# Counting edges in a metaformer kernel: stationary and moving operand exchanged, even and odd columns of words in the two column halves of the array

## The chip, the cores and the metric

The kernel runs on one core of a Trainium2 chip. The metric is the device time of one execution in microseconds (us); less is better. The core has a matrix engine (PE, with its weight loads shown as PEld), a vector engine (DVE), an engine for activations and copies (ACT), a general engine (POOL), and a sync engine (SP) that mostly issues DMAs. Each engine works through its own instructions strictly in the order in which they were written for it; engines wait for each other through semaphores.

## What is computed

The reference is a network of two layers on an image x of shape (2, 64, 64, 256): layer 0 is a deformable attention and a mixture of four experts whose router is a graph attention over 1,048,576 edges; layer 1 is a window attention and a mixture of eight experts. The part that matters here is the graph attention:

```python
M = 2 * 4096                      # 8192 nodes that exist
src = edge_index[0]; dst = edge_index[1]     # drawn from 0 .. 65535
e = leaky_relu(a_src[src] + a_dst[dst], 0.2)
ee = exp(e - e_max[dst])
denom = segment_sum(ee, dst, num_segments=M)
agg = segment_sum(h[src] * alpha[:, :, None], dst, num_segments=M)
```

Node numbers reach beyond the 8192 nodes that exist. A source out of range is read as the last node, M - 1; an edge whose destination is out of range adds to no sum. So seven of eight sources are the same node, and all edges with that source and one destination carry the same message. It is enough to count them per destination: the router multiplies the last node's message by `count`.

## The kernel before

**Stages.** `static_maps` (0 to about 990 us) computes the query, key, value and offset maps of layer 0: projections and transposes on PE (L245, L251), depthwise convolutions of queries and values on DVE (L205, L207), of keys on PE (L349), offsets on PE (L372, L373), transposes of values (L297). `static_attention` follows from 991 us with the dot products (L473) and the weighted sums (L733 to L746). Then come the router, the experts of layer 0, the attention of layer 1 and its experts.

**Sorting and counting.** `sort_edges` is a generator that `static_maps` steps through while it writes its own work, so the sorting lies among the maps of layer 0. A scheduler then fixes one order per engine. The 1,048,576 edges lie as 128 partitions of 8192 columns, taken in 16 chunks of 512 columns. Per chunk two DMAs load sources and destinations (L1077, L1078). DVE packs each edge with a destination that exists into one 32-bit word (L1079 to L1083), and picks the 56 greatest words of each 256 columns and partition, eight at a time (L1088, L1089). That makes 112 columns of words per chunk, 1792 in all (`NW`).

**One-hot products.** Bits 0 to 6 of a word are the low part of the destination (`lob`), bits 7 to 12 the high part (`hib`); a word that is no edge of the last node, or empty, gets 512 or more added to the high part and so matches nothing. For 16 columns of words (`JC`) DVE writes two one-hot tiles in bfloat16 in one instruction each: `ol` [128, 128, 16] (L1115) and `oh` [128, 64, 16] (L1116), from buffers of which there are two each. The column of words is the last index, so the operand of one column, `ol[:, :, j]`, takes every 16th element. PE then multiplies them, one matmul per column of words, all into one sum:

```python
psc = pp.tile([P, NT], F32, name="psc")          # [128, 64]
nc.tensor.matmul(
    psc, lhsT=ol[:, :, j], rhs=oh[:, :, j], start=(c1 == 0), stop=(c1 == NW - 1),
)
```

`lhsT` is the stationary operand, loaded as weights; `rhs` moves through the array. Contraction runs over the 128 partitions, so `psc[low, high]` grows by the number of words with that destination. At the end DVE copies `psc` to `count` (L1123) and goes on with the choice of the words that are not counted (L1125 to L1157: L1132 and L1133 pick the front words, L1147 finds the greatest left).

**Shape of the array.** A float32 matmul runs as two passes. The profile names for each PE instruction the shape in which the array is used, rows*columns: 128*128 for the projections, convolutions, offsets, transposes and the counting before the change; 64*64 for the small products of the offset weights (L895); 32*64 for L473; 128*64 for the logits of layer 1 (L1830), whose output goes by turns to partitions 0 to 63 and 64 to 127.

Of the kernel before, what the change touches and what calls it, by code (L numbers as in the profile page):

```python
# [23 lines left out]
F32 = mybir.dt.float32  # L24
I32 = mybir.dt.int32
AF = mybir.ActivationFunctionType
ALU = mybir.AluOpType
# [4 lines left out]
P = 128  # L32
# [3 lines left out]
NT = M // P  # L36
# [104 lines left out]
class Net:  # L141
# [905 lines left out]
    def sort_edges(self, one):  # L1047

        tc, nc, I = self.tc, self.nc, self.I
        es = I["edges"][0].rearrange("(p j) -> p j", p=P)
        ed = I["edges"][1].rearrange("(p j) -> p j", p=P)
        BF = mybir.dt.bfloat16
        NS = NCOL // SUBC  # L1060
        NW = NS * SUBK
        INSIDE = float(np.array([WORD | M], np.int32).view(np.float32)[0])
        count, front, left, dealt, rounds = one
        with tc.tile_pool(name="se1", bufs=1, side="right") as op, tc.tile_pool(name="se2", bufs=2, side="right") as wp, \
                tc.tile_pool(name="seps", bufs=1, space=PSUM, side="right") as pp:
            iota = op.tile([P, P], F32, name="iota")
            nc.gpsimd.iota(iota, [[1, P]], base=0, channel_multiplier=0, allow_small_or_imprecise_dtypes=True)
            number = op.tile([P, P, JC], BF, name="number")
            nc.vector.tensor_copy(number, iota.unsqueeze(2).to_broadcast([P, P, JC]))
            first = op.tile([P, NS, SUBK], F32, name="first")  # L1070
            rest = op.tile([P, NCOL // CHUNK + 4], F32, name="rest")
            psc = pp.tile([P, NT], F32, name="psc")
            c1 = 0
            for c0 in range(0, NCOL, CHUNK):
                si = wp.tile([P, CHUNK], I32, name="si")
                di = wp.tile([P, CHUNK], I32, name="di")
                nc.sync.dma_start(si, es[:, c0 : c0 + CHUNK])  # L1077
                nc.sync.dma_start(di, ed[:, c0 : c0 + CHUNK])  # L1078
                nc.vector.tensor_scalar(si, si, M - 1, None, ALU.min)  # L1079
                nc.vector.tensor_scalar(si, si, 13, WORD | (M - 1) << 13, ALU.logical_shift_left, ALU.bitwise_xor)  # L1080
                nc.vector.tensor_tensor(si, si, di, ALU.bitwise_or)
                wf = wp.tile([P, CHUNK], F32, name="wf")
                nc.vector.scalar_tensor_tensor(wf, di, float(M), si.bitcast(F32), ALU.is_lt, ALU.mult)  # L1083
                for k in range(CHUNK // SUBC):
                    part = wf[:, k * SUBC : (k + 1) * SUBC]
                    at = c0 // SUBC + k
                    for r in range(0, SUBK, 8):
                        nc.vector.max(first[:, at, r : r + 8], part)  # L1088
                        nc.vector.match_replace(part, first[:, at, r : r + 8], part, 0.0)  # L1089
                nc.vector.tensor_reduce(rest[:, c0 // CHUNK : c0 // CHUNK + 1], wf, AX.X, ALU.max)  # L1090
                nc.sync.dma_start(left[:, c0 : c0 + CHUNK], wf)


                n = CHUNK // SUBC * SUBK
                words = first[:, c0 // SUBC : c0 // SUBC + CHUNK // SUBC, :].rearrange("p a b -> p (a b)")
                wi = words.bitcast(I32)
                lo = wp.tile([P, n], I32, name="lo")
                hi = wp.tile([P, n], I32, name="hi")
                nc.vector.tensor_scalar(lo, wi, P - 1, None, ALU.bitwise_and)
                nc.vector.tensor_scalar(hi, wi, 7, NT - 1, ALU.logical_shift_right, ALU.bitwise_and)  # L1100
                lob = wp.tile([P, n], BF, name="lob")
                nc.vector.tensor_copy(lob, lo)

                other = wp.tile([P, n], F32, name="other")
                nc.vector.tensor_scalar(other, words, INSIDE, 512.0, ALU.is_ge, ALU.mult)
                hib = wp.tile([P, n], BF, name="hib")
                nc.vector.tensor_tensor(hib, other, hi, ALU.add)
                nc.vector.tensor_scalar(other, words, 0.0, 512.0, ALU.is_equal, ALU.mult)
                nc.vector.tensor_tensor(hib, other, hib, ALU.add)
                for j0 in range(0, n, JC):  # L1110
                    ol = wp.tile([P, P, JC], BF, name="ol")
                    oh = wp.tile([P, NT, JC], BF, name="oh")
                    lj = lob[:, j0 : j0 + JC].unsqueeze(1)
                    hj = hib[:, j0 : j0 + JC].unsqueeze(1)
                    nc.vector.tensor_tensor(ol, lj.to_broadcast([P, P, JC]), number, ALU.is_equal)  # L1115
                    nc.vector.tensor_tensor(oh, hj.to_broadcast([P, NT, JC]), number[:, 0:NT, :], ALU.is_equal)  # L1116
                    for j in range(JC):
                        nc.tensor.matmul(  # L1118
                            psc, lhsT=ol[:, :, j], rhs=oh[:, :, j], start=(c1 == 0), stop=(c1 == NW - 1),
                        )  # L1120
                        c1 += 1
                yield
            nc.vector.tensor_copy(count, psc)  # L1123
            ff = first.rearrange("p a b -> p (a b)")
            nc.vector.scalar_tensor_tensor(ff, ff, INSIDE, ff, ALU.is_ge, ALU.mult)  # L1125
            inner = op.tile([P, NS, SUBIN], F32, name="inner")
            nc.vector.tensor_copy(inner, first[:, :, 0:SUBIN])
            nc.vector.memset(first[:, :, 0:SUBIN], 0.0)
            nf = inner.rearrange("p a b -> p (a b)")
            more = op.tile([P, SPREAD + SPARE], F32, name="more")  # L1130
            for r in range(0, KEEP, 8):
                nc.vector.max(front[:, r : r + 8], nf)  # L1132
                nc.vector.match_replace(nf, front[:, r : r + 8], nf, 0.0)  # L1133
            for r in range(0, SPREAD + SPARE, 8):
                nc.vector.max(more[:, r : r + 8], nf)
                nc.vector.match_replace(nf, more[:, r : r + 8], nf, 0.0)

            nc.sync.dma_start(dealt, more[:, 0:SPREAD])
            hand = op.tile([P, SPREAD], F32, name="hand")
            nc.sync.dma_start(hand, dealt.rearrange("p c -> (p c)").rearrange("(j q) -> q j", q=P))  # L1140
            for r in range(KEEP, FRONT, 8):
                nc.vector.max(front[:, r : r + 8], hand)
                nc.vector.match_replace(hand, front[:, r : r + 8], hand, 0.0)
            at = NCOL
            for i, words in enumerate((ff, nf, hand, more[:, SPREAD:])):
                n = words.shape[1]
                nc.vector.tensor_reduce(rest[:, NCOL // CHUNK + i : NCOL // CHUNK + i + 1], words, AX.X, ALU.max)  # L1147
                nc.sync.dma_start(left[:, at : at + n], words)
                at += n
            top = op.tile([P, 1], F32, name="top")  # L1150
            nc.vector.tensor_reduce(top, rest, AX.X, ALU.max)
            topa = op.tile([P, 1], F32, name="topa")
            nc.gpsimd.partition_all_reduce(topa, top, P, bass_isa.ReduceOp.max)
            nc.vector.tensor_scalar(rounds, topa[0:1, :], 0.0, float(NLEFT), ALU.is_gt, ALU.mult)
# [1176 lines left out]
```

## Time and profile before

| what | us |
|---|---|
| median of 5 runs | 6423.25 (6404.69 to 6434.82) |
| the profiled execution's own time | 6407.83 |
| its span, first to last instruction | 6406.0 |
| PE busy | 5043.2 |
| DVE busy | 3726.7 |
| ACT busy | 1440.7 |
| POOL busy | 2263.9 |
| counting matmuls L1118, 1792 of them, busy | 239.1 |
| one-hot tiles `ol` L1115, 112 of 1.223 | 137.0 |
| one-hot tiles `oh` L1116, 112 of 0.683 | 75.5 |
| copy of the counts L1123 | 0.224 |
| key convolutions on PE L349, busy | 264.5 |
| offsets on PE L372, busy | 177.2 |
| projections on PE L251, busy | 179.8 |

How to read it: the engines work side by side, so busy times do not add up to the span. A group of instructions is a line of the kernel, an engine, an operation and the tiles it writes and reads. The duration of a matmul is from its start until its result stands; matmuls overlap in the array, so the pace of a row of them is the distance from start to start. Idle time before an instruction is put down to what released it: "DVE ol L1115 <- PE psc L1118" is DVE waiting at L1115 for the matmuls of L1118. The granted clock of PE is given as a share of full speed; it averages 0.84 over the span and is 1.00 or 0.50 at any moment of it.

### The profile page before, as it was taken

The numbers are of one execution on the slowest core, as the hardware profiler recorded it, in microseconds if no ns is written. First come the engines' busy times: TensorE is split into PE (matmuls) and PEld (weight loads), VectorE is DVE, ScalarE is ACT, GpSimd is POOL, SyncE is SP. The second block draws the span as 40 slices with busy tenths as digits, with TensorE's granted clock in tenths as the row PEclk, the third lists the DMA queues.
The fourth block names the chain that finished last, engine by engine and source line by source line (L and its number), as shares of the span: only waits on it lengthen the run. The fifth ranks groups of instructions, "written<-read, shape, count | busy, mean of one in ns | idle before, by whom it ended". The sixth has DMA issues, their size and how long they took to land. (4 is left out here: it accounts for less than half of the span.)

```text
span 6406.0 us, 68586 instructions
## 1 busy us (share of the span) xinstructions
PE 5043.2 (79%) x23911; PEld 3020.3 (47%) x23911; DVE 3726.7 (58%) x6085; ACT 1440.7 (22%) x2580; POOL 2263.9 (35%) x1994
## 2 busy tenths in 40 slices
PE   9999985698899898998772667089966777769983
PEld 5646783333334343333341333078843444448872
DVE  7797775567888888899551448012135555532223
ACT  3221112223333332310030000022213444312210
POOL 0000000247777687798417440700034111110025
PEclk9899985578898898998895878599977878879996
DMA  4446666545555555642430000267732000048875
GB/s 155 151 131 147 107 47 149 115 97 145 117 138 131 135 140 140 139 102 60 103 66 6 4 4 1 102 222 225 224 115 63 20 20 21 20 144 261 262 238 154
DMA packets 946767, 740.49 MB, mean 116 GB/s; under 512 B 611794, under 2 KB 833246, under 8 KB 935264
## 3 DMA queue, kind: packets, MB, share of 16 engines
q1 hardware_dynamic: 725004, 488.35, 30.3%
q10 hardware_dynamic: 185812, 167.81, 9.7%
q0 software_dynamic: 35584, 79.71, 4.2%
q8 instruction: 197, 3.23, 0.2%
q14 instruction: 170, 1.39, 0.1%
HBM read 469.87 MB, written 276.15 MB: 116 GB/s over the span
## 5 line engine op out<-in xcount | busy, mean ns | idle before, releaser
L746 PE MATMUL acc<-prod,ident 128*128 128x512 f32 x2716 | 1389.6, 657 | 156.5 <-POOL prod L740 129.5
L733 DVE TENSOR_TENSOR prod<-vt,wp 128x1536 f32<-128x1536 f32 (+1 forms) x796 | 1334.6, 1734 | 210.7 <-PE acc L746 156.2
L740 POOL TENSOR_TENSOR prod<-prod 128x512 f32<-128x512 f32 x1010 | 1305.9, 1316 | 418.3 <-DVE prod L733 397.8
L746 PEld LDWEIGHTS acc<-prod,ident 128*128 128x128 f32 x2716 | 524.2, 205 | 822.6 <-issue 547.5
L480 ACT COPY stage<-dot 128x384 f32<-128x384 f32 (+1 forms) x640 | 482.4, 840 | 1073.0 <-PE dot L473 905.2
L473 PE MATMUL dot<-kt,qt 32*64 32x192 f32 (+1 forms) x5888 | 514.4, 417 | 154.9 <-ACT stage L480 86.3
L1501 PE MATMUL ps_h<-xgT,w1t 128*128 128x256 f32 x2240 | 552.6, 395 | 49.1 <-DVE xgT L1496 16.7
L1234 PE MATMUL ps<-oh,ol 128*128 128x512 f32 (+1 forms) x864 | 362.2, 583 | 252.8 <-DVE oh L1227 152.0
L473 PEld LDWEIGHTS dot<-kt,qt 32*64 32x64 f32 x5888 | 281.3, 165 | 546.5 <-ACT stage L480 267.7
L1509 PE MATMUL ps_y<-w2t,hT 128*128 128x256 f32 x2240 | 512.8, 383 | 0.0
L1512 DVE TENSOR_TENSOR y<-ps_y,b2t 128x256 f32<-128x256 f32 x280 | 118.9, 425 | 654.7 <-PE ps_y L1509 494.4
L1501 PEld LDWEIGHTS ps_h<-xgT,w1t 128*128 128x128 f32 x2240 | 421.3, 195 | 133.3 <-DVE xgT L1496 27.6
L1509 PEld LDWEIGHTS ps_y<-w2t,hT 128*128 128x128 f32 x2240 | 431.7, 193 | 59.4
L1504 ACT ACTIVATE hT<-ps_h,b1t 128x256 f32<-128x256 f32 x560 | 258.3, 473 | 854.8 <-PE ps_h L1501 781.2
L1234 PEld LDWEIGHTS ps<-oh,ol 128*128 128x128 f32 x864 | 180.8, 213 | 433.9 <-issue 333.8
L2127 POOL DMA_INDIRECT xs<-tn,sloti x128 | 124.3, 971 | 646.4 <-DVE slot L2125 553.6
L1596 POOL DMA_INDIRECT back<-ys,back_row x128 | 123.2, 963 | 621.7 <-DVE run L2112 549.5
L207 DVE SCALAR_TENSOR_TENSOR cv<-pad,colt,cv 128x2048 f32<-128x2048 f32 x128 | 296.8, 2345 | 0.0
L349 PE MATMUL ps_k<-padk,diag 128*128 128x512 f32 x576 | 264.5, 613 | 20.3 <-ACT km L354 16.2
L1494 PE MATMUL ps_x<-ident,xg 128*128 128x128 f32 x560 | 85.2, 275 | 230.5 <-DMA xg<-xs 230.5
L1118 PE MATMUL psc<-oh,ol 128*128 128x64 bf16 x1792 | 239.1, 306 | 22.6 <-DVE oh L1116 22.6
L1118 PEld LDWEIGHTS <-ol 128*128 128x128 bf16 x1792 | 225.3, 148 | 53.6 <-issue 42.1
(392 smaller groups left out, 6008.4 us busy)
## 6 DMA issues: line engine op xcount, KB each, us to landing
w1t<-in_W SPq DMA_DIRECT2D x140, 512.0 KB
w2t<-in_W SPq DMA_DIRECT2D x140, 512.0 KB
xg<-xs SPq DMA_DIRECT2D x140, 256.0 KB
ys<-y ACTq DMA_DIRECT2D x140, 256.0 KB
kt<-kd SPq DMA_DIRECT2D x176, 160.0 KB
pr<-stage SPq DMA_DIRECT2D x16, 1584.0 KB
pad<-pr SPq DMA_DIRECT2D x16, 1122.0 KB
b2t<-in_b SPq DMA_DIRECT2D x140, 128.0 KB
```

The source lines that it names most:

```text
L207: nc.vector.scalar_tensor_tensor(out, src, w, out, ALU.mult, ALU.add)
L349: nc.tensor.matmul(ps.rearrange("p a b -> p (a b)"), lhsT=diag[:, tap, :], rhs=pad[:, at : at + 8, tap % 3 : tap % 3 + W], start=(tap == 0 ...
L473: nc.tensor.matmul(ps[jj][H * b : H * b + H, i, 0 : m * H], lhsT=qt[at, i0 + i, :, b], rhs=kt[at, i0 + i : i0 + i + m, b, :], start=True, ...
L480: (nc.vector.tensor_copy if alone and jj else nc.scalar.copy)(box["d"][:, 0:m, :, x : x + 2].rearrange("p s y i -> p i (s y)"), ps[jj][:, ...
L733: nc.vector.tensor_tensor(pr[:, 0:m], win, wp[:, xh, 0:m, XQ * xq : XQ * xq + XQ].unsqueeze(3).to_broadcast([P, m, XQ, HC]), ALU.mult,)
L740: nc.gpsimd.tensor_tensor(pf[:, 0], pf[:, 0], pf[:, s], ALU.add)
L746: nc.tensor.matmul(box["a"][i].rearrange("p x c -> p (x c)"), lhsT=self.ident, rhs=pf[:, s, :], start=i not in started, stop=last,)
L1118: nc.tensor.matmul(psc, lhsT=ol[:, :, j], rhs=oh[:, :, j], start=(c1 == 0), stop=(c1 == NW - 1),)
L1234: nc.tensor.matmul(psf[:, c : c + m], lhsT=ol, rhs=ohf[:, c : c + m], start=(start and j == 0), stop=(stop and j == n - 1),)
L1501: nc.tensor.matmul(ps, lhsT=w1t[:, k, f * P : (f + 1) * P], rhs=xT[:, k, :], start=(k == 0), stop=(k == CC - 1),)
L1504: nc.scalar.activation(hT[:, f, :], ps, AF.Gelu, bias=b1t[:, f : f + 1])
L1509: nc.tensor.matmul(ps, lhsT=hT[:, f, i * P : (i + 1) * P], rhs=w2t[:, f, :], start=(f == 0), stop=(f == NF - 1),)
```

## The change

The operands of the counting matmul change places: the one-hot of the high part (64 columns) becomes the stationary operand, that of the low part (128 columns) moves. The result of a matmul is then [64, 128], high by low, and takes 64 partitions. Even columns of words add into partitions 0 to 63 of `psc`, odd ones into partitions 64 to 127, which are the two column halves of the array. At the end the two sums are brought back to low by high and added: ACT copies `psc`, PE transposes it, ACT copies one half to `count`, and DVE adds the other half.

```diff
-            psc = pp.tile([P, NT], F32, name="psc")
+            psc = pp.tile([P, P], F32, name="psc")
...
                     for j in range(JC):
+                        at = NT * (c1 % 2)
                         nc.tensor.matmul(
-                            psc, lhsT=ol[:, :, j], rhs=oh[:, :, j], start=(c1 == 0), stop=(c1 == NW - 1),
+                            psc[at : at + NT], lhsT=oh[:, :, j], rhs=ol[:, :, j], start=(c1 < 2), stop=(c1 >= NW - 2),
                         )
                         c1 += 1
                 yield
-            nc.vector.tensor_copy(count, psc)
+            both = op.tile([P, P], F32, name="both")
+            nc.scalar.copy(both, psc)
+            turned = pp.tile([P, 2, NT], F32, name="turned", tag="psc")
+            nc.tensor.transpose(turned.rearrange("p a b -> p (a b)"), both, self.ident)
+            nc.scalar.copy(count, turned[:, 0])
+            nc.vector.tensor_tensor(count, count, turned[:, 1], ALU.add)
```

The tiles `ol` and `oh`, the DVE instructions that write them, the number of matmuls and all DMAs are the same. The scheduler sets the order of every engine anew for the changed program.

## The prediction

> **What bounds the kernel now.** The first question is where the counting of edges lies, and which engine sets the pace there. I read the page's slices first, then the counting line alone, then the stretch that holds it, then the waits of that stretch.
>
> ```profile
> PE   9999985698899898998772667089966777769983
> DVE  7797775567888888899551448012135555532223
> PEclk9899985578898898998895878599977878879996
> ```
>
> Each digit is 160 us. Counting (L1115 to L1120) runs in the first six and a little of the seventh: PE is at nine tenths or more, DVE at seven to eight. So PE sets the pace, with DVE close behind.
>
> ```profile
> L1118 PE MATMUL psc<-oh,ol x1792: 281/307/328, 36.6 to 994.6; 128*128 128x64 bf16 x200
> 0.00:965.00 965.00, 881.28 (x4355) 625.47 (x4356) 778.32 (x1457) 201.21 (x274) 28.30 (x27) 0.93 0.56 123
> DVE ol L1115 <- PE psc L1118: 154.4, 66, 22.6
> PE psc L1118 <- DVE oh L1116: 22.6, 6, 12.9
> ```
>
> The second line gives busy us of PE, weight loads, DVE, ACT and POOL from 0 to 965: PE has 965 - 881 = 84 us idle, DVE 187, of which 154 are waits until the counting matmuls give a buffer `ol` free. The other way round PE waits only 22.6 us for DVE. PE time saved or spent here moves DVE too.
>
> What does one counting matmul cost? Its recorded 307 ns hold its way through the array; the pace is the distance of starts.
>
> ```profile
> 44.49 2.15 PE L1118 MATMUL psc<-oh,ol 128*128 128x64 bf16 x16
> 46.46 1.04 PE L251 MATMUL ps_q<-xT,wq 128*128 128x512 f32 x2
> 47.34 2.15 PE L1118 MATMUL psc<-oh,ol 128*128 128x64 bf16 x16
> 964.97 12.30 PE L1118 MATMUL psc<-oh,ol 128*128 128x64 bf16 x96 [12.94 <-DVE oh L1116]
> ```
>
> From 44.49 to 46.46 sixteen words take 1.97 us; at 964.97 ninety-six take (12.30 - 0.31) / 95 = 126 ns each. The granted clock was 1.00 in the first stretch and 0.50 in the last, and the pace is the same. That is the fact the forecast hangs on: 125 ns is not array time. Both one-hot operands are read every 16th element of a tile [P, 128, 16] or [P, 64, 16], so 64 moving columns cost 125 / 64 = 1.95 ns each. That the moving side sets it, not the weights, shows in the single starts: the next weight load is issued 2 ns after a matmul and the next matmul 123 ns after that load. Where the weights set the pace (L895, 64 weight columns read at every ninth element, 18 moving columns) the load comes 75 ns after the matmul and the matmul 45 ns after the load, 120 ns in all, again 1.88 ns per spread-out element.
>
> **The change part by part.** *Swapped roles.* `oh` (64 columns) becomes the weights and `ol` (128 columns) the moving side. A matmul now moves 128 spread-out columns: 128 x 1.95 = 250 ns. *Two halves.* Even words go to array columns 0 to 63, odd words to 64 to 127, so two may run side by side. The trace has this form already in L1830 (128 rows, 64 columns, halves alternating):
>
> ```profile
> 5139.98 1.03 PE L1822 MATMUL ps_v<-Wv,xw 128*128 128x256 f32 x4
> 5140.93 1.08 PE L1830 MATMUL ps_s<-qm,un 128*64 128x256 f32 x8
> 5141.95 0.48 PE L1883 MATMUL ps_y<-Wo,oT 128*128 128x256 f32 x1
> ```
>
> L1822 starts a 256-column pass every 216 ns; L1830's eight begin in pairs 7 ns apart, a pair every 216 ns. Halves do overlap fully, each with its own moving data. So two words in 250 ns: 125 ns per word, what it was. The weight load of 64 columns (120 ns by L895) fits twice into 250 ns. Bounds: 54 ns per word if a half moves spread-out columns as L1830 moves close ones (128 / 256 x 216 / 2), 250 if spread-out streams do not overlap. I take 125, as L895 and L1118 show one price per element at different numbers of concurrent reads.
>
> The page "TensorEngine Tiling (Array Packing)" of the Trainium skill, section "When to Use Tiling", recommends just this swap with two column tiles where the moving side is at most 64 wide, for up to twice the speed. By that rule, as an estimate, PE would lose half of the counting, 112 us, and the kernel would end near 6370.
>
> By the row no such gain is left: the pace ignores the clock, the swap doubles the spread-out reads of each matmul, and the halves win back only that.
>
> *Switches of the array's shape.* All work around the counting uses the array as 128*128. L1822's fourth pass should be through at 5139.98 + 4 x 0.216 = 5140.84; L1830's first weight load begins at 5140.93, and its first pass lasts 430 ns where the others last 380. So going in costs 94 ns of emptying (44 cases of this pair at full clock lie at 93 to 94; 135 at half clock) and then the weight load in the open: 50 ns there, 120 here by L895. Going out costs 94 and the load of 128 columns in the open: L1883's first pass lasts 0.48 where L1822's median is 0.382, 0.10. Before, neither was paid: the counting's first load hid under the matmul ahead of it. Sum per stretch of counting: 0.094 + 0.120 + 0.094 + 0.104 = 0.41 us. In the changed program's order there are 95 stretches (97 before; 71 of both are of 16 words): 95 x 0.41 = 39 us of PE time.
>
> How much reaches the end? PE's 84 idle us hold waits for others (ACT `off` 25.9, DVE `oh` 22.6, ACT `km` 16.2), and from 300 to 500 DVE is itself at 90 to 97%; there lateness of PE is swallowed. Elsewhere DVE, ACT and the DMAs behind them wait for PE. All of it: +39; a third: +13. I take 70%: +27.
>
> *The end of counting.* DVE's copy of 0.224 us goes. For it come: an ACT copy 128x128 out of the sums (below 0.59, the time of L246's 512 columns), a transpose of two passes at half clock (213 ns apart, 0.42 long, 0.65 in all), an ACT copy of 64 columns, a DVE addition: some 1.8 us in sequence. Queued behind the addition on DVE are L1133, L1132 and the copies L480 that PE's L473 waits for; behind the ACT copies ACT's half of L480. Against it: before, DVE sat 15.3 us in front of its copy since the last 16 words stood behind the first L473; in the new order the last 112 words run in one piece ahead of it. So -10 to +2; taken as 0. SP issues the same transfers in slightly other order, POOL's order is unchanged; PE, ACT and SP are reshuffled a little (L349 against L372), for which I allow 10 us either way.
>
> **Sum.** 1792 words at no change, 39 us of switches at 70%: 6407.8 (the profiled run; span 6406.0 and 1.8 around it) + 27 = 6435. The median of the five runs shown is 6423.25, 15 above that execution, so the forecast is 6450.
>
> **Rivals.**
> *A, the forecast:* pace kept, switches paid; own range 6420 to 6480. For it: 125 ns at both clocks, 94 ns at every change of shape.
> *B, faster:* the spread-out price is not per column of a stream, but comes from weights and moving data taking turns, or the halves read better than one. Then 54 to 85 ns per word: 1792 x (125 - 54) = 127 us less, or 72, against 39 of switches: -88 or -33 of PE time. DVE's 154 us of waits would shrink, but DVE's 778 us of work soon decide, so some 60%: 6370 to 6403, taken 6385. It starts to win below 125 - 39000 / 1792 = 103 ns per word. Against it: L895 shows the same price for weights alone.
> *C, much slower:* the two moving streams take turns at one reader: 250 ns per word, 1792 x 125 = 224 us, with the switches 263; PE then decides nearly alone, 90%: 6660. Against it: L1830's pairs; for it only that those columns lie close together.
> *D, the clock:* the granted clock fell to 0.50 after stretches of 32 words (at 290 to 294 and 914 to 918), so counting hardly counts as load. Stretches grow from 2.0 to 2.4 us. A spell lasts 3.4 us and costs at most 1.7; twenty more make 34 us on top of A: 6485.
>
> **How the numbers follow.** A 0.56, B 0.23, C 0.11, D 0.10. A measurement of this kernel tells 0.3% (19 us) from no change. Three quarters of A (those above a 50% share), all of C and D are slower: 0.63. The rest of A and a little of B are within: 0.16. Faster: 0.21. The range takes A, D and the upper half of B: 6385 to 6520; C and the lower half of B, two in ten, are left out.
>
> **What will show it.** Starts of the counting matmuls: pairs some 250 ns apart mean A, below 200 B, a single one every 250 C. The first weight load of a stretch should come 94 ns after the matmul ahead has moved its columns, and PE's busy time from 0 to 965 should not fall. DVE's wait for `psc` at `ol` should grow from 154 to about 190. A granted clock well below 0.93 from 0 to 965 speaks for D. If words take under 103 ns, or the stage ends no later though switches are paid, I am wrong.

## The result, and the profile after

| | us |
|---|---|
| before, median of 50 runs beside the new ones | 6417.40 (6397.99 to 6434.82) |
| after, median of 26 runs | 6427.62 (6410.54 to 6440.24) |
| ratio after / before | 1.0017, 95% interval 1.0010 to 1.0023 |
| forecast | 6450, range 6385 to 6520, "slower by over 0.3%" at 0.63 |

The change costs 0.17% (11 us, by the interval 6 to 15). That is within the 0.3% that the forecast called no change. The sign, the pace and the price of the shape changes held; the size of the whole did not. The profiled execution of the changed kernel spans 6396.2 us, less than the 6406.0 of before. Single executions of one kernel scatter by some 15 us either way, so neither span says anything about 11 us; the distances inside the first 1000 us, which came again within some 6 us on a second chip, do.

The page of the changed kernel, busy tenths in 40 slices of 160 us:

```profile
PE   9999885698899898998782567079966777769983
DVE  7798774467888887899551448112135555532223
PEclk9999995587898897999895788589987888879996
```

PE is at eight tenths or more in the first six slices, and the granted clock in them is higher than before (999999 for 989998). The counting line by itself, weight loads and matmuls; columns are the line, the engine, output <- input, and min/median/max ns of one:

```profile
L1120 PEld LDWEIGHTS <-oh x1792: 194/199/230, 36.6 to 974.5; 128*64 128x64 bf16 x200
L1120 PE MATMUL psc<-ol,oh x1792: 411/415/502, 36.6 to 974.7; 128*64 128x128 bf16 x200
```

The shape is now 128*64 with 128 moving columns. A matmul records 415 ns for 307; the longest, up to 502, are the first pairs after a change of shape. The stretch from 0 to 965 us (busy us of PE, weight loads, DVE, ACT, POOL, then the mean granted clock), and what DVE and PE waited for in it:

```profile
0.00:965.00 965.00, 893.61 (x4388) 571.67 (x4390) 776.87 (x1462) 203.15 (x276) 31.61 (x29) 0.96 0.55 123
DVE ol L1116 <- PE psc L1120: 150.5, 58, 19.5
PE psc L1120 <- DVE oh L1117: 10.9, 5, 6.6
```

PE is busy 893.6 us for 881.3, at a clock of 0.96 for 0.93. DVE waits 150.5 us for the counting, not the 190 of the forecast.

What one stretch of counting costs can be read directly where PE alternates between 16 words and two passes of L251. Before:

```profile
97.72 2.16 PE L1118 MATMUL psc<-oh,ol 128*128 128x64 bf16 x16
99.69 1.04 PE L251 MATMUL ps_q<-xT,wq 128*128 128x512 f32 x2
100.57 2.15 PE L1118 MATMUL psc<-oh,ol 128*128 128x64 bf16 x16
```

After:

```profile
96.35 2.15 PE L1120 MATMUL psc<-ol,oh 128*64 128x128 bf16 x16
98.43 1.12 PE L251 MATMUL ps_q<-xT,wq 128*128 128x512 f32 x2
99.48 1.70 PEld L1120 LDWEIGHTS <-oh 128*64 128x64 bf16 x16 [0.76 <-issue]
99.49 2.14 PE L1120 MATMUL psc<-ol,oh 128*64 128x128 bf16 x16
101.55 1.12 PE L251 MATMUL ps_q<-xT,wq 128*128 128x512 f32 x2
```

The same work takes 100.57 - 97.72 = 2.85 us before and 99.49 - 96.35 = 3.14 after; over all such rounds of 16 words and two passes (13 to 15 of them in each of the four profiles) the medians are 2.85 and 3.13, 0.28 more. Inside it, the single starts on PE give the parts: the first weight load comes 93 to 94 ns after the matmul ahead has moved its columns (some 90 cases at full clock); the first pair of a stretch takes 312 ns, some 80 longer than the others; going out, the next weight load comes 340 ns after the last matmul started, 106 more than a pair's 234; and the first pass after it takes 0.697 us, where it took 0.612 before, 0.085 more. Together 0.37. Against that, the six pairs between the first and the last start every 233 to 235 ns instead of two words in 250, which gives back the other 0.09. One thing that was said of the engines needs a limit: PE's weight loads do not keep strictly to the written order, in which every matmul follows its own load. In the stretch at 96.35 the loads of the second pair start at 96.450 and 96.454, both ahead of that pair's first matmul at 96.666. Over 95 stretches, 94 of them ahead of the last offset matmul, 0.28 makes 26 to 27 us of PE time.

How that goes on to the end, in this pair of profiles and in a second one (both kernels once more on another chip):

| | before | after | before, second | after, second |
|---|---|---|---|---|
| last offset matmul starts | 949.4 | 958.9 | 954.6 | 964.3 |
| of it, lost to the half clock | 31.0 | 15.1 | 34.8 | 23.5 |
| half clock from 0 to 965 | 133 | 85 | 135 | 102 |
| first L473 | 991.2 | 1004.3 | 996.5 | 1010.0 |
| last dot product L473 | 2840 | 2850 | 2842 | 2853 |

"Lost to the half clock" adds up, over all float32 passes up to that matmul, how much longer each took at 0.50 than its columns take at 1.00. The last offset matmul comes 9.6 us later in both pairs. That is 26 of the stretches, less 16 (11 in the second pair) of half clock that is no longer lost, less 1 and 5 of everything else. The hand-over to L473 adds some 4 us, so that stage ends 13 us later; at the last dot product 10 to 11 of it are left, and by the medians as many at the end. The hand-over before, ACT's last offset copies and value copies, SP's store of the offsets, the first L473:

```profile
949.68 0.73 ACT L377 COPY off<-ps_off 128x306 f32<-128x306 f32 x1 [4.50 <-PE ps_off L373]
950.20 1.12 ACT L299 COPY vt<-ps_t 128x512 f32<-128x512 f32 x2
950.43 0.53 SPq L378 DMA_DIRECT2D offd<-off  x1
...
991.24 1.54 PE L473 MATMUL dot<-kt,qt 32*64 32x192 f32 x8 [13.98 <-DMA kt<-kd]
...
994.95 0.22 DVE L1123 COPY count<-psc 128x64 f32<-128x64 f32 x1 [15.28 <-PE psc L1118]
```

And after, with the new end of the counting:

```profile
957.40 1.07 ACT L299 COPY vt<-ps_t 128x512 f32<-128x512 f32 x2 [7.79 <-DMA vd<-vt]
...
963.61 1.29 ACT L377 COPY off<-ps_off 128x306 f32<-128x306 f32 x2 [5.14 <-DMA vd<-vt]
964.93 0.55 SPq L378 DMA_DIRECT2D offd<-off  x1
...
975.16 0.27 ACT L1126 COPY both<-psc 128x128 f32<-128x128 f32 x1 [10.25 <-PE psc L1120]
975.48 0.47 PE L1128 MATMUL turned<-ident,both 128*128 128x128 f32 x1 [0.36 <-ACT both L1126]
975.99 0.21 ACT L1129 COPY count<-turned 128x64 f32<-128x64 f32 x1 [0.56 <-PE turned L1128]
976.24 0.22 DVE L1130 TENSOR_TENSOR count<-count,turned 128x64 f32<-128x64 f32 x1 [0.78 <-ACT count L1129]
...
1004.29 1.98 PE L473 MATMUL dot<-kt,qt 32*64 32x192 f32 x16 [28.34 <-DMA kt<-kd]
```

Before, ACT's last offset copies stand ahead of the last value copies and start 0.3 us after PE's last offset matmul. In the scheduler's new order they stand behind them, and ACT waits 5.14 us for value stores (`vd<-vt`) first. From the last offset copy to L473 it is 41.5 us before and 40.2 after (41.6 and 40.5 in the second pair), so the delay of that copy is passed on. The counting itself is through 19 us earlier than before (976.5 for 995.2), and its four new steps take 1.3 us from 975.16 to 976.46; neither moves L473.

### The profile page after: what moved, and what is told of

Same layout as the page of the kernel before. It is cut to its first block, busy times and chain, and to the rows that moved or that the text cites. A ratio compares the mean times of both kernels' runs of the same rounds, so it can differ in the third digit from the quotient of the medians.

```text
span 6396.2 us, 68598 instructions
## 1 busy us (share of the span) xinstructions
PE 5043.2 (79%) x23912; PEld 2955.2 (46%) x23912; DVE 3719.0 (58%) x6085; ACT 1441.9 (23%) x2582; POOL 2270.0 (35%) x1994
## 5 line engine op out<-in xcount | busy, mean ns | idle before, releaser
L473 PE MATMUL dot<-kt,qt 32*64 32x192 f32 (+1 forms) x5888 | 516.2, 414 | 165.9 <-ACT stage L480 86.6
L473 PEld LDWEIGHTS dot<-kt,qt 32*64 32x64 f32 x5888 | 284.2, 164 | 554.7 <-ACT stage L480 273.7
L2193 POOL DMA_INDIRECT yt<-ye,rowi x64 | 60.7, 949 | 529.9 <-DMA xg<-xs 471.4
L1120 PE MATMUL psc<-ol,oh 128*64 128x128 bf16 x1792 | 238.6, 424 | 11.0 <-DVE oh L1117 10.9
```

The costliest lines, as they stand in the source:

```text
L473: nc.tensor.matmul(ps[jj][H * b : H * b + H, i, 0 : m * H], lhsT=qt[at, i0 + i, :, b], rhs=kt[at, i0 + i : i0 + i + m, b, :], start=True, ...
L1120: nc.tensor.matmul(psc[at : at + NT], lhsT=oh[:, :, j], rhs=ol[:, :, j], start=(c1 < 2), stop=(c1 >= NW - 2),)
```

## The experiments

The runs came in three sets, each on a chip of its own; the kernel before ran beside each (medians 6390.65, 6120.65 and 6395.16), and ratios are always to the runs on the same chip. On the second chip (shape changes alone, near with swapped roles, the two held kernels) everything is shorter, all of it behind the last L473: that part takes 3262 to 3265 us there and 3531 to 3566 on the other chips; no run shows why. Every kernel here computes the whole result; the one of the dummy products does something more, which is said there.

**Both kernels once more.** No edit.

> The kernel before once more, for a second profile of it. Theory (the change pays 29 us of shape switches up to the last offset matmul of PE and gets 11 us back from the pace of counting and 16 us from fewer spells of half clock): the spells of half clock in the first 950 us come again, some 30 us lost to them, last offset matmul near 949 us, first L473 near 991 us. Rival (the clock differs by chance from run to run): the loss to half clock differs by 10 us or more from the first profile.

> The changed kernel once more. Theory: loss to half clock near 15 us again, so 10 us or more below the kernel before; last offset matmul near 959 us and first L473 near 1004 us. Rival (chance): the loss to half clock is as in the kernel before, and the last offset matmul comes near 970 us.

Measured: 6380.64 and 6386.53, one execution each. The landmarks are in the table above: the 9.6 us at the last offset matmul, the smaller loss to the half clock and the later L473 all came again. So these are properties of the two programs and not of an execution.

**One half only.** The changed kernel with every word in the lower 64 columns.

```diff
-                        at = NT * (c1 % 2)
+                        at = 0
...
-            nc.tensor.transpose(turned.rearrange("p a b -> p (a b)"), both, self.ident)
-            nc.scalar.copy(count, turned[:, 0])
-            nc.vector.tensor_tensor(count, count, turned[:, 1], ALU.add)
+            nc.tensor.transpose(turned, both, self.ident[:NT, :NT])
+            nc.scalar.copy(count, turned)
```

> Operands exchanged as in the change, but every column of words goes to the lower half of the array, into one sum of 64 partitions. Theory (a matmul of 128 spread-out columns takes some 235 ns, and the change gains its pace only from two halves moving at once): starts 235 ns apart for each word, 1792 x 117 = 210 us more PE time than in the changed kernel, time near 6600 us. Rival (the pace is bounded by all reads together, not by the moving side of each half): starts well below 235 ns, time below 6520 us.

Measured: 6678.99, ratio 1.0452 (1.0425 to 1.0478), 288 us; the expectation had a time near 6600. The counting in one stretch, and the first 965 us:

```profile
125.44 3.98 PE L1120 MATMUL psc<-ol,oh 128*64 128x128 bf16 x16
0.00:965.00 965.00, 940.36 (x3073) 566.00 (x3074) 651.54 (x1230) 180.51 (x241) 28.33 (x27) 0.79 0.39 111
```

Sixteen words take 3.98 us for 2.15: a word every 233 ns instead of a pair. So the two halves do run side by side, fully. The clock of the stretch fell to 0.79, and the loss to the half clock rose to 109 us. Those are two causes for one slowdown, so the 288 us must not be put to the lost overlap alone.

**Shape changes alone.** The kernel before, with a product of shape 128*64 and 16 moving columns ahead of every 16 words, which nobody reads.

```diff
+            spare = pp.tile([NT, JC], F32, name="spare")
...
+                    nc.tensor.matmul(spare, lhsT=oh[:, :, 0], rhs=oh[:, 0, :], start=True, stop=True)
```

> The kernel before, with one more small matmul ahead of each 16 words (64 weight columns, 16 moving columns, into a sum of its own that nobody reads): the array changes its shape twice more per stretch, the pace, the roles and the order of all transfers stay. Theory (a change of shape there and back costs PE some 0.3 us with the open weight loads, and nearly all of it reaches the last offset matmul and with it the first L473): 112 x 0.4 = 45 us more PE time, last offset matmul 30 to 45 us later, time 25 to 45 us longer. Rival (waits of PE for others swallow the switches): time less than 12 us longer.

Measured: 6149.85, ratio 1.0055 (1.0042 to 1.0068), 34 us. Rounds of 16 words and two passes:

```profile
97.24 0.29 PE L1118 MATMUL spare<-oh 128*64 128x16 bf16 x1
97.46 2.19 PE L1120 MATMUL psc<-oh,ol 128*128 128x64 bf16 x16
99.46 1.04 PE L251 MATMUL ps_q<-xT,wq 128*128 128x512 f32 x2
100.43 0.29 PE L1118 MATMUL spare<-oh 128*64 128x16 bf16 x1
```

A round is 100.43 - 97.24 = 3.19 us, 0.34 more than before; 105 of them lie ahead of the last offset matmul, which makes 36 us. It starts at 987.2 for 949.4 and 954.6, 33 to 38 later, of which 3 to 7 are half clock (37.8 lost for 31.0 and 34.8). So 30 of the 36 arrive there, and by the ratio the end is as much later. The waits on PE swallow a sixth of such a delay, not the 30% of the forecast.

**Columns of the one-hots nearer together.** The roles of before; the tiles are laid out as [P, 16 / JI, columns, JI], so that the columns of one word are JI elements apart, 8 bytes with JI = 4, where they were 32. Same bytes written, same number of instructions.

```diff
-                    ol = wp.tile([P, P, JC], BF, name="ol")
+                    ol = wp.tile([P, JC // JI, P, JI], BF, name="ol")
...
-                            psc, lhsT=ol[:, :, j], rhs=oh[:, :, j], start=(c1 == 0), stop=(c1 == NW - 1),
+                            psc, lhsT=ol[:, j // JI, :, j % JI], rhs=oh[:, j // JI, :, j % JI], start=(c1 == 0), stop=(c1 == NW - 1),
```

> The kernel before with its operand roles, but the one-hot tiles laid out so that the columns of one word lie 4 elements (8 bytes) apart instead of 16 (32 bytes); the number of instructions and the order are the same. Theory (the pace of 125 ns is the price of spread-out moving columns): the counting matmuls start at most 80 ns apart, PE's work before 965 us falls by 80 us or more and the kernel ends 30 to 90 us earlier, unless DVE writes the tiles more slowly (1.22 and 0.68 us each now). Rival (125 ns is a floor of pairs of weight load and matmul in bfloat16): the pace stays at 125 ns and so does the time.

> Roles as before the change, one-hot columns 8 bytes apart, a second time on another chip. Both theories: about 0.983 of the kernel before, as in the first run of it, 62 ns per word. It stands here as the partner of the two steps of 4 and 16 bytes.

Measured: 6286.26, ratio 0.9830 (0.9809 to 0.9850), and on another chip 6296.23, 0.9839 (0.9820 to 0.9858): some 100 us faster, a little more than the 90 that were expected at most.

```profile
L1125 PE MATMUL psc<-oh,ol x1792: 217/243/261, 38.7 to 898.1; 128*128 128x64 bf16 x200
85.08 1.15 PE L1125 MATMUL psc<-oh,ol 128*128 128x64 bf16 x16
86.05 1.09 PE L251 MATMUL ps_q<-xT,wq 128*128 128x512 f32 x2
86.98 1.16 PE L1125 MATMUL psc<-oh,ol 128*128 128x64 bf16 x16
```

A word every (1.15 - 0.243) / 15 = 60 ns (62 in the median of all starts), for 125. The round takes 1.90 us for 2.85. The first L473 starts at 895.7. DVE writes the tiles as fast as before (1223 and 687 ns). So what bounded the counting was how far apart the columns lie, as the forecast had it, and the remedy is the layout of the tiles rather than the shape of the product.

**The same with swapped roles and both halves.**

```diff
-                            psc[at : at + NT], lhsT=oh[:, :, j], rhs=ol[:, :, j], start=(c1 < 2), stop=(c1 >= NW - 2),
+                            psc[at : at + NT], lhsT=oh[:, j // JI, :, j % JI], rhs=ol[:, j // JI, :, j % JI], start=(c1 < 2), stop=(c1 >= NW - 2),
```

> The changed kernel with the columns of one word 8 bytes apart. Theory (the price is per moving column of a half, and falls to a half at 8 bytes as it did in the kernel before, from 125 to 62 ns): pairs start 124 ns apart, 62 ns per word, the same pace as with the old roles; the 95 changes of shape remain, so 10 to 40 us slower than the old roles with 8 bytes (6286 us). Rival (two halves read better once columns lie closer): pairs below 100 ns, and the time no longer than with the old roles.

Measured: 6042.51, ratio 0.9870 (0.9855 to 0.9886).

```profile
87.00 1.15 PE L1127 MATMUL psc<-ol,oh 128*64 128x128 bf16 x16
88.09 1.12 PE L251 MATMUL ps_q<-xT,wq 128*128 128x512 f32 x2
89.14 1.15 PE L1127 MATMUL psc<-ol,oh 128*64 128x128 bf16 x16
```

Pairs every 120 to 124 ns, again two words in the time of two. The first pair of a stretch now takes 134 ns, 14 over the others, where it was 80 over them at 32 bytes: the weight load in the open is dear where the weights lie far apart. The round takes 2.14 us, 0.24 more than with the old roles. The last offset matmul comes at 869.9 for 852.5, and by the ratios, which stand against before on different chips, the end is 0.3 to 0.4% later. So at this layout too the swap brings no pace and costs the shape changes.

**Which operand, and how near.** Columns 16 bytes apart (JI = 8), 4 bytes apart (JI = 2), and 8 bytes in the moving operand alone with the weights left at 32.

```diff
-            JI = 4
+            JI = 8
```

```diff
-            JI = 4
+            JI = 2
```

```diff
-                            psc, lhsT=ol[:, :, j], rhs=oh[:, :, j], start=(c1 == 0), stop=(c1 == NW - 1),
+                            psc, lhsT=ol[:, :, j], rhs=oh[:, j // JI, :, j % JI], start=(c1 == 0), stop=(c1 == NW - 1),
```

> Roles as before, columns 16 bytes apart. Theory 1 (price per 16 bytes that are read): still 125 ns per word, and the stage ends as in the kernel before. Theory 2 (price grows with the distance between 8 and 32 bytes): some 80 to 95 ns per word.

> Roles as before, columns 4 bytes apart. Theory 1 (what one moving column costs grows with the bytes between columns, so the price is per stretch of memory read): about 31 ns per word, unless the weights' load or the array's own 64 columns at 2.4 or 1.2 per ns sets a floor (27 at full clock, 54 at half). PE would give back at most another 1792 x 31 = 55 us, but the vector engine bounds the first part by then, so the end gains 0 to 25 us on the 8-byte step. Theory 2 (a column costs one read however near the next is, and 8 bytes was merely the better of two modes): 62 ns per word and the same time as the 8-byte step. Against both: if the vector engine writes the one-hot tiles slower in runs of two, the end is later than with 8 bytes.

> Roles as before; only the moving operand has its columns 8 bytes apart, the weights keep 32. Theory of the forecast (the moving side alone sets the pace): 62 ns per word, as with both near. Rival (weights read far apart cost as much as moving data): about 125 ns per word, no change in the counting.

Sixteen words with 16 bytes, with 8 in the moving operand alone, and with 4 at full and at half clock, from three kernels:

```profile
850.45 2.10 PE L1125 MATMUL psc<-oh,ol 128*128 128x64 bf16 x16
```

```profile
88.01 1.20 PE L1124 MATMUL psc<-oh,ol 128*128 128x64 bf16 x16
```

```profile
83.62 0.65 PE L1125 MATMUL psc<-oh,ol 128*128 128x64 bf16 x16 [0.15 <-DVE oh L1121]
849.62 1.01 PE L1125 MATMUL psc<-oh,ol 128*128 128x64 bf16 x16 [0.72 <-DVE oh L1121]
```

By the median of starts a word takes 122 ns at 16 bytes, 62 at 8, and at 4 bytes 30 at full clock and 53 at half. With the moving operand alone at 8 bytes it is 65. So the price is per 16 bytes that are read and not per distance (16 and 32 bytes cost nearly the same, and from 16 down each halving of the distance halves it), it lies on the moving side, and at 4 bytes it has fallen to where the clock counts again. One execution each gave 6400.62 at 16 bytes and 6282.58 with the moving operand alone. The 4-byte kernel, over five runs: 6261.76, ratio 0.9788 (0.9770 to 0.9807), the fastest of all, 2.1% below before. On the same chip it beats the 8-byte one (0.9839), with intervals that do not meet. That gain of some 34 us was above the 25 expected at most.

**The last values held back.** Both kernels, with the last two entries in the list of value work (16 rows of values, the borders of the second map) written after the last offsets, to see what the order at the hand-over is worth.

```diff
+                late = todo.pop()
                 todo.append((borders, (1,)))
+                late = [late, todo.pop()]
...
+                for step, args in late:
+                    step(*args)
```

> The changed kernel with the last convolution of values (its transposes and stores) written after the offset loop, so that this work comes last. Its partner is the kernel before with the same edit: both then send the last stores of offsets and values in the same order. Theory (of the 13 us at the first L473 some 10 come from PE and 4 from the last offset copy standing behind the last value stores): this one 4 to 14 us slower than its partner. Rival (the whole loss comes from the order of transfers at the end of the stage): both agree within 4 us.

> The kernel before with the last convolution of values written after the offset loop: the partner of the run above. Both theories: near the kernel before, within 25 us.

Measured: 6132.74, ratio 1.0034 (1.0021 to 1.0047), with the changed kernel; 6130.25, ratio 1.0020 (1.0009 to 1.0031), with the one of before. Holding helps neither. First L473: 1009.5 and 1014.1; from the last offset copy to it 35 and 55 us, where all unheld kernels but that of the one half have 40 to 43. The edit moved more than the one thing it was to settle, since the value stores now come between the offsets and the transfers of queries and keys, and in different order in the two. The two intervals overlap. Taken by its letter, the sign of the second expectation (both agree within 4 us: 2.5 by the medians) came, and not that of the first. But the landmarks do not fit either: with swapped roles the last offset matmul starts 16 us later than in its partner (974.1 for 958.3, since the last 112 words of the counting now stand ahead of it), and yet the first L473 is 4.6 us earlier. So the two ways from the last offset copy to L473, 35 and 55 us, differ by more than the whole effect of the change. For the change itself this stays inconclusive: its 4 us of the hand-over are read from traces, and no run has taken them away.

## Why the prediction was off

**What bounds the kernel: right.** The first 965 us follow PE: the shape changes alone came out at the end, and 97 us less at the last offset matmul (852.5 at 8 bytes, for 949.4) are some 100 us less at the end.

**"128 x 1.95 = 250 ns", two halves fully side by side: right in kind, 6% off.** Pairs come every 234 ns, 1.83 per column. One half alone showed the overlap. The claim that the moving side sets the pace was shown by spreading only the weights: 65 ns. L895, whose weights cost 1.88 per element, was no proof of it: with a near moving side 128 weight columns at 32 bytes fit into 65 ns, so not every load of spread-out weights has that price. The rule of the Trainium skill, "TensorEngine Tiling (Array Packing)", section "When to Use Tiling" (its factor of up to two stands under "Theoretical Speedup"), gave 6370 by the forecast's estimate; no run here, at 32 or at 8 bytes, gained any pace by the swap beyond those 6%.

**"0.41 us per stretch": 0.37 measured.** Going in took 94 ns as priced, going out 106 for 94, the first pass 85 for 104, since a little of it (0.612 us for 0.59) had been paid before, and the open weight load 80 for 120. Net of the pace, 0.28.

**"39 us at 70%: +27": two errors that nearly cancel, by luck.** The stretches cost 27 us of PE time rather than 39, since the pace was taken too slow and the weight load too dear. The waits swallowed less than 30%: a sixth in the run of shape changes alone, 1 and 5 us of 26 here. PE's own lateness would so have brought 21 to 25 us to the end of the stage.

**The step that failed: the clock was left out of the sum, and rival D had its sign wrong.** D said "counting hardly counts as load" and saw twenty more spells in longer stretches. The half-clock time in the first 965 us fell instead, from 133 to 85 us and from 135 to 102. With that, 11 to 16 us came back, about half of the 26, and the last offset matmul starts 9.6 us later rather than 21 to 25. The other kernels with both halves at 32 bytes fit (15.5 lost in the held one, 40.0 in its partner with old roles), and one half alone lost 109. The cause of it stays open. Counted up to the last offset matmul, the half clock takes 120 to 147 us in the five profiles with the old roles at 32 or 16 bytes and 82 to 102 in the three with both halves at 32; with 8 bytes it takes 92 and 106 on the whole array and 85 on both halves. So two halves are not the only way to less of it, and whether more columns at work, the faster words or the order of the work does it was not taken apart.

**"DVE's wait for psc should grow to about 190": wrong.** It was 150.5 for 154.4, and 157.1 for 159.8 in the second pair. PE's net delay was 9.6 us, where this rested on some 36, and none of it shows in DVE's waits.

**"The end of counting, taken as 0": right.** 1.3 us in sequence, off the path, at a point that had moved 19 us forward. "10 us either way" for reshuffled engines covers the 4 us of ACT's order, whose place (offset copies behind value stores) the forecast did not name.

Rivals B and C fell by the pairs (234 ns, not below 200, not a single word every 250), and A's own range, 6420 to 6480, holds the time. Of the 22 us between 6450 and 6427.62, 16 are the change and 6 the starting point: the forecast built on a median of five, 6423.25, and that of the 50 runs is 6417.40. Of the share of 0.63 for slower by over 0.3%, 0.42 came from A, whose sum had no term that could give part of it back, and 0.21 from C and D.

## What to carry to other kernels

When a matmul's pace does not follow the granted clock, look at how its moving operand lies: a layout with the columns of one product 4 or 8 bytes apart was worth 1.6 to 2.1% here, where reshaping the product on the same layout was worth nothing. Every change of the array's shape has a price at both ends (0.37 us a stretch here), so a narrow shape pays only over long stretches: at the 16 ns that a pair gained here, an estimate from these two numbers is 23 pairs and more, and most stretches had 8. And a forecast for an engine under a gated clock needs a term for the clock with both signs.

## What the runs showed of the hardware

- Moving 64 bf16 columns takes 125 ns at 32 bytes apart, 122 at 16, 62 at 8 and 30 at 4: about 1.9 ns for each 16 bytes read, the same at granted clocks 1.00 and 0.50, down to 4 bytes, where half clock sets 53. The Trainium skill, "SBUF — State Buffer", section "Specifications (TRN2)", has lines of 16 bytes and asks for two hits on each for full bandwidth. The lines agree; two hits did not give full speed here (62 ns). Four halved that again (30), and at half clock it is then the clock that sets the pace (53, of which half would be 26.5).
- Weights spread by 32 bytes (128 columns of `ol`) load within 65 ns, behind a moving side that is near.
- The two column halves each read their own moving stream at full pace, also where the reads are far apart: a pair of words every 234 ns on two halves, one word every 233 on one half.
- The mean granted clock of the first 965 us was 0.93 with counting at 32 bytes on the whole array, 0.96 and 0.95 on both halves, 0.79 on one half alone.
